# A two-layer decoder on one core: the magnitude sums of the ternary weights begin one batch earlier, two tiles per step for the first matrix

## The chip, the cores and the metric

One NeuronCore of a Trainium2 chip runs the whole program in one launch. The metric is the device time of that launch in microseconds (us). A kernel is executed several times and the median is given. One further execution is recorded by the hardware profiler; its times are the ones that the lines below show. The engines are TensorE (PE; its weight loads are listed as PEld), VectorE (DVE), ScalarE (ACT), GpSimd (POOL) and SyncE (SP), which here only issues DMAs. ACT and POOL have DMA queues of their own as well.

## The reference

Six stages over 4 batches of 512 rows by 512 features, each followed by a residual sum and a layer norm:

```python
x = _layernorm(x + _L0_attn_ref(x, ...))            # A: one head over all 512 features, rope, softmax
x = _layernorm(x + _L0_xattn_ref(x, ctx_2048, ...)) # B: 8 heads over feature blocks
x = _layernorm(x + _L0_ffn_ref(x, ...))             # C: ternary weights, 512 -> 2048 -> 512
x = _layernorm(x + _L1_attn_ref(x, ...))            # D: 16 heads
x = _layernorm(x + _L1_xattn_ref(x, ctx_2048, ...)) # E
x = _layernorm(x + _L1_ffn_ref(x, ...))             # F: 4-bit weights, 512 -> 1408 -> 512
```

The change concerns the weights of stage C. Each of its three matrices is replaced by a ternary one whose scale comes from the mean magnitude of the whole matrix:

```python
def weight_quant(w):
    scale = 1.0 / jnp.clip(jnp.mean(jnp.abs(w)), EPS)
    wq = jnp.clip(jnp.round(w * scale), -1.0, 1.0) / scale
    return w + jax.lax.stop_gradient(wq - w)

gate = bitlinear(x, w_gate)
up = bitlinear(x, w_up)
return h_bitlinear(jax.nn.silu(gate) * up, w_down)   # h_: a Walsh-Hadamard transform first
```

So a matrix has to be read once for its mean before any of it can be quantized, and it is read a second time to be quantized. The input x, the context and the weights of the other stages have no part in this.

## The kernel before

Stages are called A to F, and a task is a stage for one batch: A0, A1, ..., F3, in that order (`ORDER`). Each task is a Python generator that emits instructions for one step and yields, a step being mostly one group of matmuls into one bank of PSUM. `lanes` keeps up to two tasks going; the next one joins when the last has said "next", so that the scores and values of one batch stand beside the projections of the following. After every round `lanes` calls `step(n)`, with n the number of tasks started, and that advances the background generators of the list `BESIDE` (L40) by one step each: an entry names the task from which it runs, the last task, and a key. Key "C0" is `l0_ffn_ternary`, key ("B", 0) loads the context for B0, key "C" is `l0_ffn_weights`, which first runs what is left of "C0".

The emitted instructions then pass through a list scheduler that orders them on each engine; every engine works its queue off in that order. A `Pipe` delays a piece of work by steps: `later(n, fn)` runs fn at the nth `tick`. A statement under `issue_after(x)` isn't placed before instruction x. Tiles come from pools with a fixed number of buffers: 69 for 128x512 tiles in general ("o"), 4 for `tw` (`W_BUFS`, L28), which hold `wk`, a weight of A, first. A `tw` load thus waits until the sum of the tile four before has read its buffer.

`l0_ffn_ternary` (L579 to L634) does the following for `wg_t`, `wu_t`, `wd_t`, each 16 tiles of 128x512 float32 (256 KB):

- It loads had16 and had, two 128x128 matrices for the Walsh-Hadamard transform (had on POOL's DMA queue, L586), and casts had on DVE (L588, recorded at L60).
- Per step it loads one tile `tw` on SP (recorded at L253), and one step later `absum` sums its magnitudes on DVE (L592).
- For the second and third matrix the matrix before is quantized beside it: `fetch` reads the tile again as `tq` on ACT's DMA queue (L602), 4 steps later ACT scales it (L555), then POOL clips it (L564), ACT casts it to bf16 (`tb`, L572), and every second step a pair of tiles is stored from ACT's queue (L597).
- After 16 tiles come the row sum on DVE (L623), a matmul with ones on PE (`tot`, L627) and two small DVE instructions (L630, L631), a step apart.

`wd_t` is quantized in `l0_ffn_weights`, from B0 on, on DVE (L558, L559) and ACT (L572).

A's own names: `qk` are projections of queries and keys, `v` values, `as` scores, `ae` their exponentials, `ap` the transposed ones, `pv` the result. A float32 product is made of three matmuls of high and low parts: the split of a tile into `...h` (a cast on ACT, L144) and `...l` (L147, on DVE or POOL) is done by one helper. B reads x from DRAM as tiles `x`, makes `qh` (ACT, L471) and `ql` (DVE, L472) of it, and its scores are `bs` (PE, L528), their exponentials `be`, the transposed ones `bT`.

In A0 the task takes 4 steps of `qk`, 4 of a product of weights, 4 of `qk` and 4 of `v`, with those of its pipe, before it says "next".

Of the kernel before, what the change touches and what calls it, by code (L numbers as in the profile page):

```python
# [21 lines left out]
B, S, D = 4, 512, 512  # L22
# [14 lines left out]
F_SCALED, F_ACT, F_PAIR, F_DOWN = 1, 5, 3, 9  # L37
ORDER = "A0 A1 A2 A3 B0 B1 B2 B3 C0 C1 C2 C3 D0 D1 D2 D3 E0 E1 E2 E3 F0 F1 F2 F3"

BESIDE = [("A1", "A3", "C0"), ("A3", "B0", ("B", 0)), ("B0", "B2", "C"), ("C3", "D0", "D"), ("D1", "D3", "F0"), ("E2", "E2", "F")]  # L40


class Pipe:
# [25 lines left out]
class Net:  # L69
# [509 lines left out]
    def l0_ffn_ternary(self):  # L579


        nc = self.nc
        self.had = self.c("had", [P, P], F32R)
        self.had16 = self.load(self.c("had16", [P, P]), self.a["had16"])
        f = self.t("had")
        nc.gpsimd.dma_start(f[:, 0:P], self.a["had"])  # L586
        pipe = Pipe()
        pipe.later(3, nc.vector.tensor_copy, self.had, f[:, 0:P])  # L588

        def absum(f, part, n):  # L590
            with self.tc.issue_after(self.mark.ins):
                nc.vector.tensor_reduce(part[:, n : n + 1], f, AX.X, ALU.add, apply_absolute_value=True)  # L592


        def store(name, n, o):
            with self.tc.issue_after(self.turned.ins):
                nc.scalar.dma_start(self.tern_kept[name][n], o.bitcast(F32))  # L597

        def fetch(ap):
            f = self.o("tq")  # L600
            with self.tc.issue_after(self.turned.ins):
                nc.scalar.dma_start(f, ap)  # L602
            return f

        def keep(name, n, o):
            pipe.later(1, store, name, n, o)

        old = None
        for new in self.TERNARY:
            chunks = self.ternary_chunks(new)  # L610
            part = self.c(new + "_abs", [P, len(chunks)])
            if old:
                quant = self.ternary(pipe, old, lambda n, o, name=old: keep(name, n, o), early=True)
                todo = self.ternary_chunks(old)
            for n in range(len(chunks)):
                pipe.tick()
                pipe.later(1, absum, self.load(self.w("tw"), chunks[n][2]), part, n)
                if old:
                    pipe.later(4, quant, n, fetch(todo[n][2]))
                yield  # L620
            pipe.tick()
            m = self.c(new + "_mean", [P, 4])
            nc.vector.tensor_reduce(m[:, 2:3], part, AX.X, ALU.add)  # L623
            yield
            pipe.tick()
            ps = self.pb("tot")
            nc.tensor.matmul(ps[:, 0:1], self.ones, m[:, 2:3], start=True, stop=True)  # L627
            yield
            pipe.tick()
            nc.vector.tensor_scalar(m[:, 0:1], ps[:, 0:1], 1.0 / (len(chunks) * P * 512), 1e-5, ALU.mult, ALU.max)  # L630
            nc.vector.reciprocal(m[:, 1:2], m[:, 0:1])  # L631
            self.mean[new], self.scale[new] = m[:, 0:1], m[:, 1:2]
            old = new
        yield from pipe.drain()  # L634
# [699 lines left out]
def body(tc, args, phases=range(6)):  # L1334
    with ExitStack() as ctx:
# [9 lines left out]
        def step(n):  # L1345
            if len(phases) == 6:
                for first, last, key in BESIDE:
                    if plain.index(first) < n <= plain.index(last) + 1:
# [74 lines left out]
```

## Time and profile before

| | us |
|---|---|
| three runs | 1580.09, 1582.03, 1579.72 |
| their median | 1580.09 |
| the profiled execution | 1580.57 |
| its span on the core | 1578.9 |

The span is the time from the first to the last instruction; the profiled execution's own time is 1.7 us longer. The mean granted clock of PE is 0.994 of full speed. What the ternary weights cost one by one, in this execution:

| instruction | engine | number | mean us | where in the span |
|---|---|---|---|---|
| `tw` load (256 KB) | SP queue | 48 for the sums | lands in 3.5 to 4.0 | wg 23.0 to 99.2, wu 100.5 to 163.3 |
| L592 sum of magnitudes | DVE | 48 | 0.67 | wg 48.5 to 104.6, wu 105.8 to 169.8, wd 189.3 to 227.9 |
| L602 fetch `tq` (256 KB) | ACT queue | 32 | 0.33 to issue, lands in 4.1 (wg) and 4.8 (wu) | |
| L555 scale | ACT | 32 | 0.72 | the most of them in 160 to 242.7, the last four after 242.4 |
| L572 cast to bf16 | ACT | 32 (and 4 for wd in this stretch) | 0.62 | with those |
| L597 store | ACT queue | 16 | 0.33 to issue | |

Windows of stage A, one row per stretch: from and to, its length, the busy time of PE, PEld, DVE, ACT and POOL with the number of instructions, the granted PE clock, the share of the DMA engines, GB/s:

```profile
40.00:56.80 16.80, 16.80 (x75) 13.91 (x75) 8.66 (x12) 5.49 (x10) 14.46 (x11) 1.00 0.12 36
56.80:68.00 11.20, 11.20 (x51) 9.27 (x50) 4.12 (x7) 5.22 (x12) 8.86 (x7) 1.00 0.01 3
88.00:113.00 25.00, 25.00 (x115) 20.72 (x114) 20.26 (x34) 8.78 (x16) 15.60 (x11) 1.00 0.71 231
160.00:242.70 82.70, 80.72 (x368) 65.16 (x366) 61.54 (x100) 53.29 (x101) 66.27 (x58) 1.00 0.79 254
```

Other times in A: A0's first `as` follows the projections, and its third `as` tile starts at 67.71 us. A1's first `pv` starts at 96.81, its first `as` at 113.13, and A2's first `qk` at 124.76. The first xT tile is issued at 1.69 us and first read at 4.66. DVE waited for `tw` four times between 99.8 and 108.9 (0.64, 1.55, 0.60 and 1.01 us); L555 on ACT waited once for a `wg_t` fetch (3.8 us) and four times for `wu_t` fetches in 215 to 260 (7.1 us in all, 2.4 the longest). A3's last `ap` ends at 242.73, B0's first `bT` starts at 267.97.

### The profile page before, as it was taken

The numbers are of one execution on the slowest core, as the hardware profiler recorded it, in microseconds if no ns is written. First come the engines' busy times: TensorE is split into PE (matmuls) and PEld (weight loads), VectorE is DVE, ScalarE is ACT, GpSimd is POOL, SyncE is SP. The second block draws the span as 40 slices with busy tenths as digits, with TensorE's granted clock in tenths as the row PEclk, the third lists the DMA queues.
The fourth block names the chain that finished last, engine by engine and source line by source line (L and its number), as shares of the span: only waits on it lengthen the run. The fifth ranks groups of instructions, "written<-read, shape, count | busy, mean of one in ns | idle before, by whom it ended". The sixth has DMA issues, their size and how long they took to land.

```text
span 1578.9 us, 25669 instructions
## 1 busy us (share of the span) xinstructions
PE 1512.4 (96%) x8222; PEld 1090.9 (69%) x8222; DVE 1214.0 (77%) x2594; ACT 1041.7 (66%) x2240; POOL 687.8 (44%) x704
## 2 busy tenths in 40 slices
PE   8999998999999999999999999999999999999996
PEld 6888775555544764477777668777687677787885
DVE  6486688898876678777577797767886898888896
ACT  5334667888778877887696864969634445545554
POOL 6665783656535303430435323353324344344342
PEclk9999999999999999999999999999999999999998
DMA  7044874444224534753434345633336630020101
GB/s 256 29 160 140 266 235 151 156 165 139 71 74 126 189 132 131 208 180 130 134 101 120 103 140 148 173 96 91 130 119 220 233 113 12 20 81 1 54 1 54
DMA packets 138759, 200.72 MB, mean 127 GB/s; under 512 B 17776, under 2 KB 52592, under 8 KB 138624
## 3 DMA queue, kind: packets, MB, share of 16 engines
q1 hardware_dynamic: 127584, 178.03, 35.5%
q10 hardware_dynamic: 6912, 12.59, 2.8%
q0 software_dynamic: 4128, 8.46, 2.2%
q8 instruction: 65, 1.06, 0.3%
q14 instruction: 70, 0.57, 0.1%
HBM read 121.94 MB, written 51.90 MB: 110 GB/s over the span
## 4 chain that ended last, share of the span: by engine, by line
PE 50%; DVE 11%; ACT 9%; issue 6%; DMA 3%; POOL 2%; SPq 0%; ACTq 0%; DVEq 0%; POOLq 0%
PE fg L1238 7%; PE facc L1221 5%; DVE fg L1194 3%; PE dT L986 3%; PE dn L794 2%; PE bo L500 2%; PE pg L740 2%; ACT de L976 2%; PE pu L742 2%; PE do L1006 2%; PE bT L249 2%; PE had L808 2%; PE bs L528 2%; PE ds L961 2%; PE dq L155 1%
## 5 line engine op out<-in xcount | busy, mean ns | idle before, releaser
L1194 DVE SCALAR_TENSOR_TENSOR fg<-fg,gs,fg 128x512 f32<-128x512 f32 x220 | 163.1, 745 | 30.4 <-ACT fg L1186 15.6
L976 ACT ACTIVATE de<-de,dm 128x128 f32<-128x128 f32 (+3 forms) x256 | 142.8, 562 | 11.5 <-DVE dm L972 11.3
L1238 PE MATMUL fg<-fxh,gu 128*128 128x512 f32 x352 | 140.4, 399 | 6.2 <-DVE fg L1194 3.1
L972 DVE CUSTOM_DVE_ANT_0 de<-ds,negm,thr 128x128 f32<-128x128 f32 (+3 forms) x256 | 126.3, 546 | 18.4 <-PE ds L961 15.8
L1238 PE MATMUL fg<-fxl,gu 128*128 128x512 f32 x352 | 137.5, 391 | 0.1
L717 POOL TENSOR_TENSOR hl<-g,hh 128x512 fp32r<-128x512 f32 x64 | 83.2, 1307 | 110.8 <-ACT hh L716 90.7
L484 POOL TENSOR_SCALAR be<-be,bsm 128x512 f32<-128x512 f32 x128 | 93.4, 742 | 85.3 <-DVE bsm L482 53.7
L1198 POOL TENSOR_TENSOR fg<-fg,fg 128x512 f32<-128x512 f32 x44 | 60.1, 1367 | 140.3 <-DVE fg L1194 56.7
L478 ACT ACTIVATE be<-bs,bsm 128x512 f32<-128x512 f32 x128 | 87.3, 689 | 32.4 <-DVE bsm L476 31.0
L898 POOL TENSOR_TENSOR dql<-dqf,dqh 128x512 fp32r<-128x512 f32 x32 | 41.4, 1295 | 150.6 <-ACT dqh L897 150.5
L986 PE MATMUL dT<-ident,de 128*128 128x128 f32 x640 | 91.3, 278 | 8.4 <-ACT de L976 6.4
L986 PEld LDWEIGHTS dT<-ident,de 128*128 128x128 f32 x640 | 71.7, 141 | 27.5 <-ACT de L976 14.8
L1238 PEld LDWEIGHTS fg<-fxh,gu 128*128 128x128 f32 x352 | 66.0, 188 | 30.6 <-DVE fg L1194 13.5
L476 DVE TENSOR_REDUCE bsm<-bs 128x1 f32<-128x512 f32 x128 | 83.0, 674 | 2.3 <-PE bs L528 2.3
L249 PEld LDWEIGHTS bT<-ident,be 128*128 128x128 f32 x512 | 54.9, 141 | 29.5 <-issue 15.6
L1238 PEld LDWEIGHTS fg<-fxl,gu 128*128 128x128 f32 x352 | 66.2, 188 | 12.8 <-DVE fxl L147 0.4
L1186 ACT ACTIVATE fg<-fg,gs 128x512 f32<-128x512 f32 x88 | 60.1, 683 | 20.6 <-PE fg L1238 20.6
L249 PE MATMUL bT<-ident,be 128*128 128x128 f32 x512 | 71.2, 280 | 1.4 <-POOL be L484 0.9
L500 PE MATMUL bo<-bpT,cT 128*64 128x512 f32 x256 | 71.4, 618 | 1.0 <-ACT bpT L491 1.0
L1212 POOL TENSOR_TENSOR fhl<-fg,fhh 128x512 fp32r<-128x512 f32 x44 | 58.5, 1330 | 29.9 <-ACT fhh L1211 29.7
L740 PE MATMUL pg<-qT,tb 128*128 128x512 bf16 x256 | 66.8, 381 | 4.4 <-ACT qT L702 2.8
L1190 ACT ACTIVATE fg<-fg,gs 128x512 f32<-128x512 f32 x44 | 30.3, 689 | 60.5 <-PE fg L1238 60.4
(357 smaller groups left out, 4685.3 us busy)
## 6 DMA issues: line engine op xcount, KB each, us to landing
x<-x SPq DMA_DIRECT2D x176, 256.0 KB, 3.2
had_scratch<-hw SPq DMA_DIRECT2D x64, 256.0 KB, 2.3
z<-had_scratch SPq DMA_DIRECT2D x64, 256.0 KB, 5.9
stk<-dqh SPq DMA_DIRECT2D x192, 64.0 KB, 2.1
tw<-in_wd_t SPq DMA_DIRECT2D x32, 256.0 KB, 4.0
p<-in_gu_p SPq DMA_DIRECT2D x22, 256.0 KB, 3.1
gu_codes<-gu SPq DMA_DIRECT2D x22, 256.0 KB, 3.1
gu<-gu_codes SPq DMA_DIRECT2D x22, 256.0 KB, 4.6
```

What stands on the lines that cost most here:

```text
L249: self.nc.tensor.transpose(pt[:, i * P : (i + 1) * P], srcs[i][:, j * P : (j + 1) * P], self.ident)
L476: nc.vector.tensor_reduce(sm[:, h : h + 1], ps, AX.X, ALU.max, negate=True)
L478: nc.scalar.activation(e, ps, AF.Exp, bias=sm[:, h : h + 1], accum_out=sm[:, 2 + h : 3 + h])
L484: nc.gpsimd.tensor_scalar(es[h][i], es[h][i], sm[:, 4 + h : 5 + h], 1.0, ALU.mult, ALU.mult)
L500: nc.tensor.matmul(po[0][h * 64 : h * 64 + 64, :], cT[j][:, c : c + 64], pTs[h], start=j == 0, stop=j == NT - 1)
L717: nc.gpsimd.tensor_tensor(lo, g, hi.bitcast(F32), ALU.subtract)
L740: nc.tensor.matmul(pg, tern["wg_t"][k, c][:, m], qT[k], start=k == 0, stop=k == NT - 1)
L972: nc.vector.tensor_tensor_reduce(es[i], ps, self.negm[:, 384 - P * i :], -1.0, self.thr[:, i : i + 1], ALU.add, ALU.min, n4[:, i : i + 1])
L976: nc.scalar.activation(es[i], es[i], AF.Exp, bias=n4[:, i : i + 1], scale=-1.0, accum_out=den[:, hh * 4 + i : hh * 4 + i + 1])
L986: nc.tensor.transpose(pt[:, o + (i - j) * P : o + (i - j + 1) * P], es[i][:, j * P : (j + 1) * P], self.ident)
L1194: self.emitted["DVE"] = nc.vector.scalar_tensor_tensor(y[u], ps, s, y[u], ALU.mult, ALU.add)
L1238: nc.tensor.matmul(ps, self.gu[i, u][:, g * P : (g + 1) * P], xT[g][n], start=n == 0, stop=n == 1)
```

## The change

The background generator of the ternary weights is advanced from A0 on instead of A1. It first yields 10 times, after its loads of had16 and had. For the first matrix, `wg_t`, the pipe ticks only at even tiles and the generator yields only after odd ones, so that two tiles are loaded and summed per step. The second and third matrix go as before, one tile per step.

```diff
-BESIDE = [("A1", "A3", "C0"), ("A3", "B0", ("B", 0)), ("B0", "B2", "C"), ("C3", "D0", "D"), ("D1", "D3", "F0"), ("E2", "E2", "F")]
+BESIDE = [("A0", "A3", "C0"), ("A3", "B0", ("B", 0)), ("B0", "B2", "C"), ("C3", "D0", "D"), ("D1", "D3", "F0"), ("E2", "E2", "F")]
...
+        for _ in range(10):
+            yield
         old = None
         for new in self.TERNARY:
             chunks = self.ternary_chunks(new)
...
             for n in range(len(chunks)):
-                pipe.tick()
+                if old or n % 2 == 0:
+                    pipe.tick()
                 pipe.later(1, absum, self.load(self.w("tw"), chunks[n][2]), part, n)
                 if old:
                     pipe.later(4, quant, n, fetch(todo[n][2]))
-                yield
+                if old or n % 2:
+                    yield
             pipe.tick()
```

The 16 tiles of `wg_t` thus take steps 11 to 18 of A0, and A1 starts at about step 20. No instruction is added or removed on any engine. What the order of the engines' queues shows: had's DMA on POOL moves from 45.9 us in the profile of before to tenth place in POOL's queue, ahead of A0's work there; had's cast moves from 49.6 us to third place on DVE; `tot` for `wg_t` stands before A0's third `as` tile on PE, that for `wu_t` among A1's `ap`, that for `wd_t` in A3's `qk`. On ACT, between A3's last `v` casts and B0's `qh`, no instruction of the ternary weights is left; on DVE none between `vl` and the first `bsm` of B0.

## The prediction

> **What bounds the kernel now.** I read the page's first two parts, then the waits of TensorE (PE) over the first 300 us, then the stretches around the longest of them, then the timelines of PE and ACT there.
>
> ```profile
> PE 1512.4 (96%) x8222; PEld 1090.9 (69%) x8222; DVE 1214.0 (77%) x2594; ACT 1041.7 (66%) x2240; POOL 687.8 (44%) x704
> ...
> PE   8999998999999999999999999999999999999996
> PEld 6888775555544764477777668777687677787885
> DVE  6486688898876678777577797767886898888896
> ACT  5334667888778877887696864969634445545554
> ```
>
> PE is busy for 1512.4 of 1578.9 us, so time comes back only where PE idles or runs slowly. One slice is 39.5 us. DVE and ACT have room in slice 2 (4 and 3 tenths, 39.5 to 79 us); in the seventh, 237 to 276.3, PE has the only 8 besides the first slice and the end.
>
> ```profile
> PE qk L155 <- ACT wqh L144: 6.0, 1, 6.0
> PE bs L528 <- ACT qh L471: 3.7, 1, 3.7
> PE pv L157 <- DVE apl L147: 1.4, 2, 0.9
> PE as L156 <- DVE qkl L147: 0.5, 1, 0.5
> PE qk L156 <- POOL xTl L147: 0.5, 2, 0.3
> ```
>
> Columns: total us, times, longest. After the start, the one large wait is that of B0's first scores (`bs`) for `qh`, at the step from A3 to B0. Windows there (length; busy us of PE, PEld, DVE, ACT, POOL; granted PE clock; DMA share; GB/s):
>
> ```profile
> 238.00:242.73 4.73, 4.73 (x31) 3.97 (x29) 2.72 (x9) 2.57 (x6) 1.14 (x2) 1.00 1.01 347
> 242.73:246.44 3.71, 0.00 (x0) 0.00 (x1) 3.29 (x9) 3.71 (x8) 2.63 (x3) 0.91 0.82 165
> 246.44:249.00 2.56, 2.56 (x10) 1.77 (x12) 1.25 (x2) 1.57 (x3) 0.35 (x2) 0.50 1.04 393
> 249.00:252.30 3.30, 3.30 (x10) 2.15 (x7) 2.77 (x6) 3.30 (x8) 0.39 (x1) 0.50 0.88 294
> ...
> 320.00:440.00 120.00, 118.42 (x713) 61.85 (x714) 105.01 (x228) 100.57 (x251) 69.59 (x92) 1.00 0.34 117
> ```
>
> PE idles 3.71 us, then has half the clock for 5.86 us. The last row, B's steady state, is PE-bound at full clock, so what is saved here is saved to the end. What kept `qh`, from ACT's timeline:
>
> ```profile
> 242.40 0.72 ACT L555 ACTIVATE tq<-tq,wu_t_mean 128x512 f32<-128x512 f32 x1
> ...
> 243.03 0.62 ACT L572 ACTIVATE tb<-tq 128x512 bf16<-128x512 f32 x1
> 243.55 0.71 ACT L555 ACTIVATE tq<-tq,wu_t_mean 128x512 f32<-128x512 f32 x1
> 244.16 0.61 ACT L572 ACTIVATE tb<-tq 128x512 bf16<-128x512 f32 x1
> 244.68 0.57 ACT L144 CAST aph<-ap 128x512 fp32r<-128x512 f32 x1
> ...
> 245.15 0.72 ACT L555 ACTIVATE tq<-tq,wu_t_mean 128x512 f32<-128x512 f32 x1
> 245.77 0.62 ACT L471 ACTIVATE qh<-x 128x512 fp32r<-128x512 f32 x1
> ```
>
> Between `ap`'s end (242.73) and `qh` ACT quantizes `wu_t`; x for B0 was loaded at 171.33 and is not what is late.
>
> **Part by part.** No instruction comes or goes: each engine has the same rows in both programs. What moves is about one batch earlier: 48 `tw` loads (SP), 48 magnitude sums (L592, 0.67 us), 32 `tq` fetches and 16 stores on ACT's queue (0.33 us to issue), 32 each of L555 (0.72), L564 (POOL) and L572 (0.62), three rounds of L623, L627, L630, L631, and the load and cast of `had`.
>
> *At A3 to B0 (gain).* In the changed program ACT's order there is vh, vh, aph, qh, aph, qh, aph, qh, aph, without ternary work. Between 242.40 and `qh`'s start stand three L555 and two L572: 3×0.72 + 2×0.62 = 3.4 us. Without them the last vh ends near 242.5 (241.92 + 0.59); `aph` needs the first `ap` tile (PE, before 242), so `qh` runs from 243.1 at the latest, from 242.05 at best (right after the vh that ends there in either order). PE then idles about 0.3 us instead of 3.71 (bounds 0 and 1.0; the upper is 243.1 + 0.62 − 242.73): −3.4. The half clock follows only the long idle: 5.86 us at 0.50 lose 2.93 us; with 0.3 idle it should not come, as 0.9 us waits elsewhere (`pv` for `apl`, above) leave the clock whole: −2.9. The last bound of the gain: `ap`'s end to the first `bT` takes 25.24 us, in which 6 score groups of 0.89 and 4 `pv` tiles of 2.95 need 17.1, so 8.1 us at most can come back here; 6.3 are named, and of the other 1.8 (waits for `apl` and single `bs`, whose ACT part also thins) I take 0.5. Sum −6.8; bounds −8.1 and 0 (if something else is as late).
>
> *What is late next.* After `qh`, `ql` (DVE 0.68) and `aph`/`apl`. DVE has no L558/559 in between any more, only vl and apl, so `ql` of the first group is there within 1 us of `qh`; a remaining stall of that size is in the bounds.
>
> *A0 (cover).* 16 sums are 16×0.67 = 10.8 us of DVE in 40 to 62 us, where DVE is idle 8.1 of 16.8 (40.00:56.80) and 7.1 of 11.2 (56.80:68.00). Four `tw` buffers and 3.5 us to land pace them: the mean is ready near 62.6, its PE `tot` stands in PE's order before the third `as` tile, 67.7 before: about 5 us to spare. DVE's next, `asm`, is some 1.75 us late in that stretch and is absorbed by the idle time. If the cover is gone, PE waits at `tot`: price its lateness, 0 here, up to 2 if tiles land twice as slowly (3.5 → 7).
>
> *A1 (the risk).* Here `wg_t` is fetched and quantized and `wu_t` summed. SP's `tw` loads pass x-transposed loads, and ACT's queue gets fetches ahead of the casts of A2's xT. DVE does ten sums in a row (6.7 us) paced by the four buffers, ending near 104; then `apl` at 105 to 106.3, which PE wants at 107. On ACT the two L555 of the first fetches wait for DMA (`tq` takes 4.1 us: issued 104.7 and 106.6, usable 108.8 and 110.7), and three casts queue behind them; they end at 112.6 to 113.7 and PE wants them at 114.5 and 115.2. Slack 0.2 to 1.6 us: I take +0.5, bounds 0 and 4 (two waits, each 2 us longer, as the longest wait of an L555 for its fetch in 215 to 260 was 2.4). This kind of clog exists in before between A2 and A3: 160 to 242.7 holds 80.72 of 82.7 PE-busy, 2.0 us. It moves into A1/A2 and leaves A3: net 0, bounds −2 and +2.
>
> The row for transfers is 238.00:242.73, share 1.01 at 347 GB/s, with `tq` landing in 4.1 to 4.8 us and `tw` in 3.5. The Trainium skill, "Trainium Kernel Development and Optimization", section "Key Constraints", says that transfers from SP's, ACT's and POOL's queues share 16 engines and interleave; that speaks against this change, since A1 already shows 0.71 share (88.00:113.00) and gets `tq` on top. By that rule alone the 0.5 would be an estimate of 1 to 2 us.
>
> *Start.* `had` (64 KB, POOL queue, 0.73 us to issue, 2.2 to land) and had16 go out ahead of the first loads; 128 KB at 350 GB/s (as 347 above) are 0.37 us, half of it in the first loads' way: +0.2. Its cast (L60, 0.22 us) is now DVE's third instruction, ahead of wql (5.99 in before); the DMA goes out at 1.5 to 2.2 and lands at 4.4, or 7.1 at the slowest (4.9, had16's): blocks DVE 0 to 1.3 us. I take 0.
>
> *B0, B1.* wd's quantization begins sooner and two L558/L559 pairs (0.9 us each) leave B's steady stretch, where DVE is busy 105.01 of 120 and PE bounds: 0, bounds −0.5 and 0.
>
> Sum: −6.8 + 0.5 + 0 + 0.2 + 0 = −6.1. Against the profiled execution (1580.57; span 1578.9 and 1.7 around it) 1574.5; the median, 1580.09, is 0.5 lower, so about 1574.3 between the two readings.
>
> **On the clock.** The row is 3.71 us idle, then 5.86 us at 0.50. The Trainium skill, "TensorE: Matmul & The Clock Gate", "Part 1: The HAM clock gate", has the clock halved after an idle window of about 3.4 us and whole again after about as long busy. By it the half clock would cost an estimated 1.7 us instead of 2.9 and the total would be near 1575.5.
>
> **Rivals.** A measurement here can tell about 0.2% from no change: 3.2 us, so 1576.9 and 1583.3 are the limits.
>
> 1. *The gain is given back.* Either `qh` or `ql` is late for another reason (A3's last `ap` casts, four `apl` on DVE in a row), or one stall in A1 is long enough to halve the clock too: 3.7 + 2.9 = 6.6. For: A1's slack is at most 1.6 us. Against: ACT has no ternary work at the step, and a 6.6 needs the casts 3.7 us later than I make them. −6.1 + 2 to −6.1 + 6.6: 1576.5 to 1581, centre 1579.
> 2. *ACT's queue clogs twice (the slower side).* Fetched tiles come late in A1 and again in A2, each time ACT stands at L555 while xT's casts wait behind it, PE idles 3.7 us or more and gets half the clock: 2×6.6 − 6.1 = +7.1, 1587.5. It decides from where A2's and A3's first xT casts come 3.7 us after PE wants them. For: an L555 in before waited 3.8 us for a `wg_t` fetch, and 7.1 in four waits for `wu_t`. Against: the same load on A2 and A3 in before cost 2.0 us up to 242.7, without half clock.
> 3. *Nothing changes at B0*, because the list order is kept: excluded by the changed order of ACT; only as part of rival 1.
>
> **How the numbers follow.** Forecast 0.68 (own range 1571.5 to 1576.9), rival 1 0.16, rival 2 0.16. Of rival 1, 0.03 lies below 1576.9, 0.11 within the limits and 0.02 above; of rival 2 0.14 above and 0.02 within. Faster 0.71, same 0.13, slower 0.16. Range 1571.5 (the −8.1 of the transition, plus 0.2, minus 0.7 elsewhere) to 1582: 0.05 lies below, 0.15 above.
>
> **What would show it.** Right: the PE wait for `qh` under 1 us, no window at 0.50 around 240, first `bT` about 18 to 20 us after the last `ap`, `tot` for `wg_t` without a wait in A0, and PE waits of 0 to 2 us in 88 to 125. Wrong: a wait of PE over 3 us or a clock under 0.9 in A1 or A2, a first `qk` more than 1 us later than before, or ACT waiting for `tq` with xT's casts behind it.

## The result and the profile after

The changed kernel is slower, by about half a per cent. Its five times are 1584.96, 1587.43, 1589.93, 1593.87 and 1594.07 us, median 1589.93, against 1580.09 of five runs of the kernel before beside them: ratio 1.0061, 95% interval 1.0033 to 1.0088. Measured again, it gave 1584.42 against 1577.02, ratio 1.0046 (1.0031 to 1.0062); both intervals lie above 1. Why the first five times spread over 9 us stays open. The forecast was 1574.3, faster.

The profiled execution (1584.96) has a span of 1583.2 us. From its page, busy time and the slices, as for the kernel before:

```profile
PE 1512.2 (96%) x8222; PEld 1091.7 (69%) x8222; DVE 1222.8 (77%) x2594; ACT 1039.6 (66%) x2240; POOL 688.2 (43%) x704
...
PE   8999899999999999899999999999999999999996
...
DVE  6685787888876688877567797767786888888896
```

PE has the same 1512 us of work. The 8 of the seventh slice (237 to 277 us) is a 9 now, and the fifth (158 to 198) has become an 8. The 8 of the seventeenth is no effect of the change: a second profile of the kernel before (r_before below) has it as well. PE's waits in the first 300 us (total us, times, longest):

```profile
PE qk L155 <- ACT wqh L144: 6.9, 2, 6.4
PE as L156 <- DVE qkl L147: 5.1, 3, 3.8
PE pv L157 <- DVE apl L147: 4.0, 2, 3.4
PE as L155 <- ACT qkh L144: 0.7, 1, 0.7
PE pv L155 <- ACT aph L144: 0.3, 1, 0.3
PE bs L528 <- DVE ql L472: 0.2, 1, 0.2
```

The wait of 3.7 us for `qh` has become one of 0.2 for `ql`. In its place stand two of 3.8 and 3.4 us, for low parts that DVE makes: `qkl` (low part of the projected queries and keys, for A2's scores) and `apl` (low part of A2's transposed exponentials, for `pv`, beside A3's projections). Windows of the changed kernel around them (length; busy PE, PEld, DVE, ACT, POOL; granted clock; DMA share; GB/s):

```profile
170.00:175.00 5.00, 4.93 (x22) 3.75 (x20) 5.00 (x6) 2.14 (x5) 4.84 (x4) 1.00 0.83 264
175.00:180.00 5.00, 0.58 (x2) 0.27 (x2) 5.00 (x8) 3.42 (x8) 4.67 (x6) 0.79 0.83 280
180.00:185.00 5.00, 5.00 (x12) 3.85 (x13) 3.61 (x7) 1.53 (x3) 4.76 (x6) 0.52 0.82 228
...
220.00:225.00 5.00, 3.93 (x17) 2.60 (x15) 5.00 (x5) 3.25 (x6) 5.00 (x4) 1.00 0.78 237
225.00:230.00 5.00, 2.38 (x6) 1.90 (x7) 4.27 (x6) 1.25 (x3) 5.00 (x5) 0.57 0.36 135
230.00:235.00 5.00, 5.00 (x18) 4.01 (x17) 4.88 (x7) 0.98 (x2) 5.00 (x4) 0.74 0.00 0
```

In both places DVE is busy for all or nearly all of the time and POOL too, PE idles, and afterwards PE works some 5 us at half the clock (the traces have it at 0.50 from 177.9 to 184.8 and from 225.7 to 232.6). What was one late tile at the step from A3 to B0 has become two. The step itself is clean, as ACT's timeline of the changed kernel shows:

```profile
254.96 0.59 ACT L144 CAST vh<-v 128x512 fp32r<-128x512 f32 x1 [2.08 <-PE v L157]
255.44 0.60 ACT L144 CAST aph<-ap 128x512 fp32r<-128x512 f32 x1
255.92 0.64 ACT L471 ACTIVATE qh<-x 128x512 fp32r<-128x512 f32 x1
```

To see where time went, PE's timeline is cut at the first `ap` transpose of each batch and at B0's first `bT`. The table has both kernels, each in two profiles (the second ones are r_before and r_after below), in us:

| stretch | before | again | after | again | after − before |
|---|---|---|---|---|---|
| start to A0's first `ap` | 81.3 | 80.7 | 82.0 | 81.3 | +0.6 to +0.7 |
| to A1's | 42.8 | 42.8 | 45.5 | 46.2 | +2.7 to +3.4 |
| to A2's | 72.4 | 72.5 | 77.9 | 79.5 | +5.5 to +7.0 |
| to A3's | 44.0 | 43.7 | 49.3 | 49.2 | +5.3 to +5.5 |
| to B0's first `bT` | 27.3 | 27.2 | 19.2 | 19.2 | −8.0 to −8.1 |
| the rest | 1310.9 | 1309.4 | 1309.2 | 1308.8 | −1.7 to −0.6 |

The gain at the step was had in full, 8 us. It was paid for with 14 to 17 us in A0 to A3, and A2 and A3 are the larger part.

### The profile page after: what moved, and what is told of

It reads as the page before. It is cut to its first block, busy times and chain, and to the rows that moved or that the text cites. A ratio compares the mean times of both kernels' runs of the same rounds, so it can differ in the third digit from the quotient of the medians.

```text
span 1583.2 us, 25665 instructions
## 1 busy us (share of the span) xinstructions
PE 1512.2 (96%) x8222; PEld 1091.7 (69%) x8222; DVE 1222.8 (77%) x2594; ACT 1039.6 (66%) x2240; POOL 688.2 (43%) x704
## 4 chain that ended last, share of the span: by engine, by line
PE 57%; DVE 16%; ACT 12%; issue 7%; DMA 4%; POOL 3%; SPq 0%; ACTq 0%; DVEq 0%; POOLq 0%
PE fg L1243 7%; PE facc L1226 5%; PE dT L991 3%; DVE fg L1199 3%; PE bo L500 2%; ACT de L981 2%; PE pg L745 2%; PE dn L799 2%; PE bT L249 2%; PE pu L747 2%; PE do L1011 2%; PE ds L966 2%; ACT be L478 2%; PE bs L528 1%; DVE bsm L476 1%
## 5 line engine op out<-in xcount | busy, mean ns | idle before, releaser
L991 PEld LDWEIGHTS dT<-ident,de 128*128 128x128 f32 x640 | 71.7, 141 | 27.5 <-ACT de L981 14.8
```

Of the source, the lines that this page charges most:

```text
L991: nc.tensor.transpose(pt[:, o + (i - j) * P : o + (i - j + 1) * P], es[i][:, j * P : (j + 1) * P], self.ident)
```

## The experiments

Theory D: DVE works its queue in order, and what the change puts in front of the splits that PE waits for (sums, scalings) costs, by its length or because its tile has not landed. Rival P: POOL's rope products (those of `z` with the rotary factors, and their sums) set the pace in A2 and A3, and DVE would wait for them anyway. Each kernel was compared with the kernel before on its chip; these have medians from 1576.7 to 1578.5 us. All in one table, in us; the stretches are those above, each from its batch's predecessor (A1 is "to A1's first `ap`"), and come from one profile each:

| kernel | median | ratio to before (95%) | A1 | A2 | A3 | step | rest |
|---|---|---|---|---|---|---|---|
| e1_hold_wd | 1578.57 | 0.9999 (0.9984 to 1.0014) | 50.3 | 77.3 | 42.9 | 19.4 | 1308.2 |
| e2_short_wd_sums | 1588.49 | 1.0070 (1.0043 to 1.0098) | 47.0 | 79.8 | 47.4 | 19.3 | 1308.4 |
| e3_short_wu_clips | 1584.03 | 1.0041 (1.0029 to 1.0052) | 46.2 | 79.6 | 47.3 | 19.2 | 1311.0 |
| e4_first_only | 1584.84 | 1.0043 (1.0028 to 1.0059) | 42.7 | 72.3 | 49.5 | 27.6 | 1309.6 |
| e5_hold_lag3 | 1580.84 | 1.0021 (1.0009 to 1.0033) | 46.8 | 79.4 | 42.9 | 19.3 | 1310.4 |
| e6_hold_sp_fetch | 1579.04 | 1.0009 (0.9997 to 1.0021) | 46.3 | 74.1 | 45.8 | 19.3 | 1311.2 |
| e8_before_late_quant | 1578.01 | 1.0004 (0.9994 to 1.0015) | 42.8 | 73.3 | 45.1 | 19.3 | 1315.0 |
| e9_hold_k18 | 1577.77 | 1.0003 (0.9992 to 1.0014) | 43.0 | 80.3 | 43.0 | 19.3 | 1313.1 |
| r_after | 1584.42 | 1.0046 (1.0031 to 1.0062) | 46.2 | 79.5 | 49.2 | 19.2 | 1308.8 |
| f1_hold_lag3_k18 | 1578.15 | 1.0003 (0.9993 to 1.0012) | 43.0 | 74.5 | 48.0 | 19.4 | 1309.0 |
| f2_hold_lag3_sp | 1580.93 | 1.0025 (1.0014 to 1.0035) | 46.7 | 76.9 | 46.9 | 19.3 | 1308.0 |
| f3_lag3_short_both | 1592.9 (one execution) | | 48.0 | 74.2 | 60.4 | 19.3 | 1308.0 |
| g1_two_early | 1581.32 | 1.0030 (1.0018 to 1.0042) | 45.1 | 72.5 | 44.1 | 28.9 | 1306.8 |
| g2_hold_k22 | 1584.96 | 1.0055 (1.0038 to 1.0073) | 44.0 | 77.7 | 48.0 | 20.1 | 1312.1 |
| g3_hold_wg_fetch_late | 1581.27 | 1.0027 (1.0014 to 1.0040) | 42.7 | 80.1 | 46.8 | 19.3 | 1308.0 |
| r_before | 1578.19 | 1.0002 (0.9989 to 1.0016) | 42.8 | 72.5 | 43.7 | 27.2 | 1309.4 |
| h1_before_pairs4_hold | 1578.81 | 1.0010 (0.9996 to 1.0023) | 42.8 | 72.5 | 45.5 | 21.5 | 1312.0 |
| h2_before_pairs8_hold | 1575.93 | 0.9994 (0.9983 to 1.0005) | 42.9 | 72.4 | 43.9 | 25.4 | 1309.0 |

### A3: wd_t's scaling

```diff
+                with self.tc.issue_after(self.low[False].ins):
-                nc.vector.tensor_scalar(f, f, self.scale[name], MAGIC, ALU.mult, ALU.add)
+                    nc.vector.tensor_scalar(f, f, self.scale[name], MAGIC, ALU.mult, ALU.add)
```

> The changed kernel, with the first scaling of each wd_t tile (L558 of the changed kernel) not placed before the last high/low split on DVE that was emitted before it; this takes four pairs of L558/L559 out of A3's projections (207 to 214 us in the changed kernel, 6.8 us of DVE there) and leaves the rest of DVE's order as it is. Theory D (DVE is too full in A2 and A3): PE's wait of 3.4 us for apl near 224 goes to under 1 us, the half clock at 225 to 232 goes, and the span falls by 4 to 6 us against the changed kernel's profiled 1583.2. Rival P (POOL's rope products set the pace there, DVE would wait for them anyway): a wait of 2.5 us or more stays and the span moves by less than 2.

The wait for `apl` near 224 is gone, A3 falls from 49.3 to 42.9 us, and the median is that of the kernel before, 6 to 11 us under the changed kernel's. The order of all engines up to the end of A3 is otherwise that of the changed kernel, so the whole loss of A3 is these four pairs. ("The held kernel" is this one below.) The span fell by 3.2 where 4 to 6 were expected, because this profile's A1 was 4.8 us longer than the changed kernel's first. That isn't the edit's doing, since A1 has the same order: here two fetches landed 0.9 and 1.9 us later, PE waited 1.6 us for `qkh` where it had not waited, and its clock was at half from 119.8 to 126.6. DVE's timeline of the changed kernel shows what the hold took away:

```profile
207.53 2.94 DVE L558 TENSOR_SCALAR tw<-tw,wd_t_mean 128x512 f32<-128x512 f32 x2
210.39 2.27 DVE L559 TENSOR_SCALAR tw<-tw 128x512 f32<-128x512 f32 x2
212.59 0.86 DVE L558 TENSOR_SCALAR tw<-tw,wd_t_mean 128x512 f32<-128x512 f32 x2
213.37 0.75 DVE L559 TENSOR_SCALAR tw<-tw 128x512 f32<-128x512 f32 x2
```

Two scalings take 2.94 us while POOL works on the rope products and 0.86 when it does not. They are emitted in B0, but `wd_t`'s mean is ready at 203 us in the changed kernel, where it came at 241.6 before, and the scheduler places them in A3.

### A2: sums, clips, late tiles

Two cuts, each on the changed kernel: the sums of `wd_t` over 8 of 512 columns, and POOL's clips of `wu_t` on 8 of 512; the rest of that work is left out.

```diff
+                g = f[:, 0:8] if "wu_t" in self.scale else f
-                nc.vector.tensor_reduce(part[:, n : n + 1], f, AX.X, ALU.add, apply_absolute_value=True)
+                nc.vector.tensor_reduce(part[:, n : n + 1], g, AX.X, ALU.add, apply_absolute_value=True)
```

> The changed kernel, with the 16 magnitude sums of wd_t taken over 8 of the 512 columns (most of their work is left out; loads, order and waits stay). Theory D: seven of these sums stand before the split qkl that PE waits 3.8 us for at 176 to 180; without them the wait is under 1.2 us, the half clock at 180 to 185 goes, and the span falls by 4 to 6 us. Rival P: qkl is late because POOL's join of the rope products is late; the wait stays above 2.5 us and the span falls by less than 2.

```diff
+                g = f[:, 0:8] if name == "wu_t" else f
-                nc.gpsimd.tensor_scalar(f, f, MAGIC + 1.0, MAGIC - 1.0, ALU.min, ALU.max)
+                nc.gpsimd.tensor_scalar(g, g, MAGIC + 1.0, MAGIC - 1.0, ALU.min, ALU.max)
```

> The changed kernel, with POOL's 16 clips of wu_t (L564) done on 8 of the 512 columns (the rest of wu_t stays unclipped). Rival P: POOL is busy for 31 of 40 us in 160 to 200, so without the clips the joins come earlier, PE's wait for qkl in 170 to 185 falls under 1.2 us and the span by 4 to 6. Theory D: the wait stays above 2.5 us, the span falls by less than 2.

Neither helped: the wait for `qkl` was 5.6 us with the short sums, and 3.3 plus 2.8 with the short clips. Both theories fail as they were put. DVE's timeline of e2_short_wd_sums tells why the first one did:

```profile
177.18 0.21 DVE L593 TENSOR_REDUCE wd_t_abs<-tw 128x1 f32<-128x8 f32 x2
182.04 0.16 DVE L593 TENSOR_REDUCE wd_t_abs<-tw 128x1 f32<-128x8 f32 x1 [4.65 <-DMA tw<-in_wd_t]
182.12 0.98 DVE L147 TENSOR_TENSOR qkl<-z,qkh 128x512 fp32r<-128x512 f32 x1
```

The sum itself is 0.16 us now, but it stands ahead of `qkl` in DVE's queue and waits 4.65 us for its tile. With full sums DVE is busy over the same stretch:

```profile
172.49 3.79 DVE L236 TENSOR_SCALAR x<-x,ln 128x512 f32<-128x512 f32 x3
176.20 0.67 DVE L147 TENSOR_TENSOR vl<-v,vh 128x512 fp32r<-128x512 f32 x1
176.80 1.86 DVE L592 TENSOR_REDUCE wd_t_abs<-tw 128x1 f32<-128x512 f32 x3
178.57 1.28 DVE L147 TENSOR_TENSOR qkl<-z,qkh 128x512 fp32r<-128x512 f32 x1
```

(changed kernel.) So the theory was widened (W): an entry whose tile has not landed counts as much as one that takes long. Tests on the held kernel: sums of the second and third matrix emitted three steps after their loads; second reads issued by SP.

```diff
-                pipe.later(1, absum, self.load(self.w("tw"), chunks[n][2]), part, n)
+                pipe.later(3 if old else 1, absum, self.load(self.w("tw"), chunks[n][2]), part, n)
...
+            for _ in range(2 if old else 0):
+                pipe.tick()
+                yield
             pipe.tick()
             m = self.c(new + "_mean", [P, 4])
```

> The held kernel (e1_hold_wd) with the magnitude sums of wu_t and wd_t emitted three steps after their loads instead of one, so that on DVE none stands ahead of the splits while its tile is still on its way. Theory W (DVE and ACT work in order, and a sum or a scaling whose tile has not landed holds up the splits behind it): PE's wait for qkl in A2's scores, 4.8 us with e1_hold_wd, goes under 1.5 us, and the median falls by 3 to 5 us against e1_hold_wd, to 1573 to 1576. Rival P (POOL's joins of the rope products are late of themselves): a wait over 2.5 us stays and the time moves by less than 2 us.

```diff
-                nc.scalar.dma_start(f, ap)
+                nc.sync.dma_start(f, ap)
             return f
```

> The held kernel (e1_hold_wd) with the 32 second reads of wg_t and wu_t issued from SP's queue instead of ACT's. Theory W: in A1 the first two fetches are issued only at 106 to 109 us because ACT waited 9.6 us for PE ahead of them; from SP they go out earlier, the first two scalings (L555) wait under 1 us together instead of 7.4, and what A1 loses up to A2's first projection (3 to 7 us) falls under 2. Rival Q (SP's queue is held up as well, by loads that wait for a free buffer): the scalings wait 3 us or more, loads of x or x-transposed come later and the time is 2 us or more above e1_hold_wd.

With the later sums the waits for `qkl` fell to 1.5 and 0.7, but 2.5 us for `xTl` from POOL came after them and halved the clock: A2 stayed at 79.4 and the time did not fall, a miss. With SP's fetches A2 fell to 74.1 (wait 1.9). A1 took 46.3, as in the changed kernel: its wait for `apl` grew to 1.7, and a scaling on ACT still waited 6.4 us for its tile, since SP issued that fetch only at 108.8; this too is a miss. The time is within noise of e1_hold_wd. Together:

> The held kernel with both changes of before, the second reads from SP's queue and the sums three steps after their loads. Theory W: the waits add up to under 4 us between 100 and 240 (8.2 with e1_hold_wd, 7.7 with e6_hold_sp_fetch, 7.7 with e5_hold_lag3), the first bT comes at 263 to 266 us, and the time is 1574 to 1577. Rival: DVE's and POOL's work in A1 and A2 is what is too much, whatever the queue; the waits stay at 6 us or more and the time at 1578 to 1581.

A2 76.9, a wait of 3.6 for `qkl` again, waits of 7.7 in all, 1580.93: the rival's numbers. And all at once, late sums, short sums, short clips, without the hold:

> The changed kernel (without the hold on wd_t's scaling) with the sums of wu_t and wd_t three steps after their loads, the sums of wd_t over 8 of the 512 columns and POOL's clips of wu_t on 8 of 512 columns; most of the work of these sums and clips is left out. Cutting one of the two alone left PE's wait for qkl in A2 at 5.6 and 6.0 us. Theory W+P (sums, clips and late tiles hold up the same chain, so that each alone only uncovers the next): the waits between 170 and 190 add up to under 1 us, while that for apl near 224 stays over 2 us, since wd_t's scaling still stands in A3. Rival: something else is late there (x-transposed tiles, ACT), and over 2.5 us stay.

2.1 us were left in A2, where under 1 was expected. A3 took 60.4 us; PE's line there, and DVE's before it:

```profile
236.79 0.79 PE L157 MATMUL pv<-vh,apl 128*128 128x512 f32 x1 [12.52 <-DVE apl L147]
```

```profile
226.38 2.88 DVE L558 TENSOR_SCALAR tw<-tw,wd_t_mean 128x512 f32<-128x512 f32 x2
229.19 2.89 DVE L559 TENSOR_SCALAR tw<-tw 128x512 f32<-128x512 f32 x2
232.00 1.48 DVE L558 TENSOR_SCALAR tw<-tw,wd_t_mean 128x512 f32<-128x512 f32 x1
...
234.65 1.48 DVE L559 TENSOR_SCALAR tw<-tw 128x512 f32<-128x512 f32 x1
236.05 0.68 DVE L147 TENSOR_TENSOR apl<-ap,aph 128x512 fp32r<-128x512 f32 x1
```

Here the four pairs, at 1.5 us for each instruction, stand right in front of the last `apl`: e1_hold_wd's finding again, larger.

That A2's loss is the third matrix's work at all is shown by leaving the second where the change has it and only sending the third back, 18 empty steps after the second:

```diff
             old = new
+            if new == "wu_t":
+                for _ in range(18):
+                    pipe.tick()
+                    yield
```

> The changed kernel with 18 empty steps after the second matrix: wg_t and wu_t are summed as in the changed kernel and wg_t quantized as there, wu_t is quantized and wd_t summed as late as in the kernel before. Theory D (the loss in A2 is the third matrix's sums and the second's quantization standing there, that in A3 wd_t's scaling): A1 loses 2 to 3 us up to A2's first projection as in the changed kernel (127.5 to 128.5 there), then A2 loses nothing, PE's waits between 165 and 235 stay under 2 us together, and the wait for qh at the step to B0 is back with 3 to 4 us; time 1579 to 1583. Rival: A2's wait follows from A1 being late, and over 3 us of it stay.

A1 45.1, A2 72.5 as before, the step back at 28.9 with a wait of 5.5 us for `qh` (3 to 4 were expected). The rest is as expected, and the rival falls. DVE's busy time over 30 us around A2's scores is 21.5 before (150 to 180 us) and 28.8 after (154 to 184), POOL's 25.5 and 27.5; sums of the windows, before and then after:

```profile
sum 30.00, PE 28.95 PEld 22.70 DVE 21.48 ACT 15.67 POOL 25.45; mean PE 4.83 PEld 3.78 DVE 3.58 ACT 2.61 POOL 4.24
```

```profile
sum 30.00, PE 25.51 PEld 20.34 DVE 28.75 ACT 15.59 POOL 27.53; mean PE 4.25 PEld 3.39 DVE 4.79 ACT 2.60 POOL 4.59
```

Which piece of that work holds `qkl` stays open: sums, clips, late tiles and POOL's splits took one another's place. Counted from `ap` to `ap`, A2 has 14 magnitude sums in both kernels, but 22 scalings, 21 clips and 22 casts after where 16, 16 and 14 stood before. The number alone does not set the loss: e6_hold_sp_fetch has 14 sums, 19 scalings, 20 clips and 20 casts there and takes 74.1.

### A1: fetches ahead of the casts

```diff
             old = new
+            if new == "wg_t":
+                for _ in range(18):
+                    yield
```

> The changed kernel, with 18 empty steps after the first matrix, so that wg_t is summed in A0 as in the changed kernel while wu_t and wd_t are summed and wg_t and wu_t quantized in the steps of the kernel before. Theory D: the loss comes from the second and third matrix moving, so here only the start's 0.4 us is lost, PE waits for qh at the step from A3 to B0 by 3 to 4 us as before, and the time is 1579 to 1582. Rival S (the sums in A0 and their transfers are what costs): 1584 or more, with PE late by 2 us or more at A1's first scores.

A1 and A2 are as before, 42.7 and 72.3, so the sums in A0 cost nothing but the start: rival S falls. The time is 1584.84 all the same, the rival's number and a miss, but from another place: A3 takes 49.5. There the sums of `wd_t` and the fetches and scalings of `wu_t` stand in another order than before, a sum waits 2.7 us for its tile with `qkl` behind it, a cast on ACT 4.3 us for `kf` (a tile of B's context), and PE waits 1.8 for `aph` and 2.3 for `apl`. ACT's timeline of the changed kernel in A1:

```profile
105.05 0.62 ACT L144 CAST qkh<-z 128x512 fp32r<-128x512 f32 x1 [9.57 <-PE v L156]
105.94 0.33 ACTq L602 DMA_DIRECT2D tq<-in_wg_t  x1
...
107.26 0.37 ACTq L602 DMA_DIRECT2D tq<-in_wg_t  x1
111.59 0.73 ACT L555 ACTIVATE tq<-tq,wg_t_mean 128x512 f32<-128x512 f32 x1 [4.21 <-DMA tq<-in_wg_t]
113.70 0.72 ACT L555 ACTIVATE tq<-tq,wg_t_mean 128x512 f32<-128x512 f32 x1 [1.38 <-DMA tq<-in_wg_t]
114.33 1.12 ACT L144 CAST xTh<-xT 128x512 fp32r<-128x512 f32 x2
```

ACT stands 9.6 us at a cast that a matmul of PE's `v` releases (in the kernel before a cast stood 10.1 us there too, with no fetch behind it); only then do the fetches go out, and ACT stands at their scalings with `xTh` and `qkh` behind. Moving the fetches 10 steps later, the sums left alone:

```diff
+                    go = lambda n=n, quant=quant, todo=todo: pipe.later(4, quant, n, fetch(todo[n][2]))
-                    pipe.later(4, quant, n, fetch(todo[n][2]))
+                    if old == "wg_t":
+                        pipe.later(10, go)
+                    else:
+                        go()
```

> The held kernel (e1_hold_wd) with the second reads of wg_t and their quantization 10 steps later, the sums where they are. Theory T (in A1 ACT stands at scalings whose tile is still on its way, the casts of x-transposed and the splits behind it): A2's first projection comes under 126.5 us (132.5 with e1_hold_wd, 127.9 in the changed kernel, 124.8 before) and the only wait left in A1 is that for apl, under 1.2 us. Rival D1 (the ten sums of wu_t in a row on DVE are what costs A1): 127.5 or later.

A2's first `qk` came at 125.8 us and A1 at 42.7: the ten sums in a row, which are still there, were not the matter; the fetches and scalings of `wg_t` were, by the waits on ACT that the timeline shows. The work then stood in A2 (80.1), where PE waited 2.7 us for `xTh`.

### Smaller shifts, and the gain alone

With 18 and 22 empty steps at the start (for 10), on the held kernel, and 18 with the later sums:

```diff
-        for _ in range(10):
+        for _ in range(18):
             yield
```

> The held kernel (e1_hold_wd) with 18 empty steps at the start in place of 10, so that the sums of wg_t end in A1 and the second and third matrix move 10 steps instead of 18. Theory W: only where the sums and fetches fall against the batch's scores counts; ACT's order at the step from A3 to B0 is as clean as with 10, and A1 gets no fetch before its scores, so the waits in A1 fall under 1.5 us; the time is 1572 to 1577. Rival (any earlier start costs the same 5 to 8 us in A2 and A3): 1579 to 1584.

> The held kernel with 18 empty steps (e9_hold_k18) and the sums of the second and third matrix three steps after their loads. With e9_hold_k18 DVE waited 4.8 us for a tile of wd_t at 167.7, the splits behind it, and PE 5.2 us for qkl. Theory W: DVE waits for no tile, PE's wait there is under 1.5 us, the first bT comes at 262 to 264 us (267.7 with e9_hold_k18, 268.0 before). If stage B passes that on, the time is 1572 to 1574; if it takes most of it back, as it did with e8_before_late_quant, 1575 to 1578. Rival P (POOL): the wait stays above 3 us.

> The held kernel with 22 empty steps, so that the second and third matrix move 6 steps. Theory D: A1 and A2 are as in the kernel before or lose under 2 us, ACT has two casts of wu_t left before the values of A3, none between them and qh, and the first bT comes at 261 to 265 us (268.0 before); the time 1573 to 1577. Rival: a wait of 3 us or more in A2 as with 18 steps, time 1577 to 1580.

None came within its expected time, the first two by under 1 us. In the first (1577.77) a sum waited 4.8 us for its tile and PE 5.2 for `qkl` (A2 80.3); the later sums removed this (74.5), and A3 lost 3.1 to `apl` behind a sum that waited 2.2 us. With 22, A1's `ap` waited 3.5 for exponentials and A3's values 2.5. Each shift has its pile-up elsewhere; none beats the kernel before.

The gain alone, in the kernel before: the last 8 tiles of `wu_t` fetched and quantized 14 steps later; then the third matrix by pairs of tiles, from the fifth and from the ninth (the second diff; 8 for 4 in the last):

```diff
+                    go = lambda n=n, quant=quant, todo=todo: pipe.later(4, quant, n, fetch(todo[n][2]))
-                    pipe.later(4, quant, n, fetch(todo[n][2]))
+                    if old == "wu_t" and n >= 8:
+                        pipe.later(14, go)
+                    else:
+                        go()
```

```diff
+                pair = new == "wd_t" and n >= 4
-                pipe.tick()
+                if not pair or n % 2 == 0:
+                    pipe.tick()
...
-                yield
+                if not pair or n % 2:
+                    yield
```

> The kernel before, with only the last 8 tiles of wu_t fetched and quantized 14 steps later, in B0, so that ACT has no ternary work between A3's last value casts and B0's first qh; nothing is moved earlier. This prices the gain of the step from A3 to B0 by itself. Theory G (that step is worth 6 to 8 us and the changed kernel paid for it in A1 to A3): PE's wait for qh under 1 us, no half clock after it, first bT 17 to 19 us after the last ap, the time 1571 to 1575. Rival B (the wait comes back in B0, where the quantization now stands, or the gain was never there): 1577 to 1582.

> The kernel before, with two tiles per step from the fifth tile of wd_t on (its sums and wu_t's quantization end 6 steps sooner) and wd_t's first scaling held behind the splits as in e1_hold_wd; A0 to A2 are untouched. Theory D (only what stands in front of PE's splits costs): A1 and A2 as in the kernel before (42.9 and 72.4 us from the first ap of one batch to that of the next), A3 44 to 46, the step to B0 19 to 20 instead of 27.4; the first bT at 260 to 263 us and the time 1570 to 1574. Rival: pairs of tiles in A3 overfill DVE, ACT and POOL there, A3 takes 48 us or more and the time is 1575 to 1580.

> As the run above, but with pairs only from the ninth tile of wd_t on (4 steps sooner); DVE's order up to the end of the sums is then that of the kernel before, and two casts of wu_t still stand between the first and second qh. Theory D: A3 44 to 45 us, the step to B0 20 to 22, the first bT at 261 to 264 us, the time 1571 to 1575. Rival: A3 48 us or more, or the step still 25, the time 1576 to 1580.

The first took the step to 19.3 us and `bT` to 261.9, 6.1 earlier than in the first profile of the kernel before and 4.9 than in the second; from there to stage C's first `pg` product it took 195.4 us where the kernel before took 190.0 and 191.4, and the median did not move: the gain is real, and B, where the eight quantizations now stand, took most of it back. The second had the step at 21.5 and `bT` 4.7 earlier, the third 25.4 and 3.1. All three missed their times: none has an interval below 1, and the best, 0.9994, is no difference. Why the 3 to 5 us of the last two do not show is not settled; up to the first `pg` they still had 2.3 and 2.7 us, and twelve times of one kernel scatter over 6 to 8.

> The kernel before once more, for a second profile. Theory G: the wait for qh at the step to B0 is there again with 3.5 to 4 us and the half clock after it, and the first bT at 267 to 269 us; what differs between two profiles of one kernel comes from stage C on. Rival: the wait in the first profile was one of a scatter, and here it is under 2.5 us, which would explain why taking it away did not show in the median of e8_before_late_quant.

> The changed kernel once more, unaltered, for a second profile and more times. Its first five times lay between 1584.96 and 1594.07, those of the kernel before within 3.3 us. Theory H (waits of PE of 3 to 4 us, each of which halves its clock or just does not): the same two waits, for qkl near 176 and for apl near 224, of 3 to 5 us each, plus the wait in A1, their sum larger than the 8.7 us of the first profile if the time is larger. Rival: the waits in A1 to A3 are as in the first profile and the scatter comes from later stages.

The second profiles repeat the first: 3.8 us for `qh` before; 4.8 for `qkl` and 3.4 for `apl` after. Of the 2.7 us between the two profiles of the kernel before, 1.2 lie ahead of B0's first `bT`, where none was expected.

## Why the prediction was wrong

- *What bounds the kernel, and that only waits and the clock of PE count:* right. The same 1512 us of PE work before and after.
- *The step from A3 to B0, −6.8 with bounds −8.1 and 0:* right in mechanism, and too small: −8.0 to −8.1 (−7.9 from A3's last `ap`, as the prediction counts: 25.24 us before, 17.33 after). Of the 1.8 us of which it took 0.5, 1.6 came. `qh` follows `aph` at once, the half clock is gone, and nothing else was late there.
- *Start +0.2, A0 at nothing:* +0.6 to +0.7 together; no wait for `tot`. The start is 0.4 of it (first `qk` at 6.4 us for 6.0).
- *A1 +0.5, bounds 0 and 4:* right in mechanism, +2.7 to +3.4. The mis-sized term is the landing of the two fetches that ACT waits for: 4.1 us were taken, 5.6 and 6.4 it was, and they were issued 1.2 and 0.7 us later than assumed, so the scalings could start at 111.6 and 113.7 where 108.8 and 110.7 stood in the sum. With the same order in A1, e1_hold_wd's profile lost 7.5 us there, beyond the bound of 4, with half the clock, which rival 1 had named.
- *"It moves into A1/A2 and leaves A3: net 0, bounds −2 and +2":* the first step that failed. A2 lost 5.5 to 7.0. The clog of the kernel before was taken as a thing that moves with its batch and keeps its price. In the kernel before twelve sums of `wu_t` and the quantization of `wg_t` stand in A2, which takes 72.4 us; with `wd_t`'s sums and `wu_t`'s quantization there instead, and what is left of `wg_t`'s, it takes 77.9 and 79.5, and with those two sent back 72.5 (g1_two_early). So this work costs A2 5 to 7 us, at waits for `qkl` of 3.8 and 4.8 with half the clock after. Which part of it, and in what order against the splits, is not shown. The prediction's own sign of being wrong, a wait over 3 us or a clock under 0.9 in A2, is what came.
- *"B0, B1: wd's quantization begins sooner and two L558/L559 pairs leave B's steady stretch: 0":* the second that failed. The pairs were costed in B, where the source emits them; in the order of DVE's queue the first four stand in A3's projections, before A2's last `apl`, and take 6.6 us of DVE there. Price: A3's 5.3 to 5.5 us, all of it (e1_hold_wd).
- *What is saved at the step goes to the end:* mostly. The rest after the first `bT` is 1307 to 1313 us in all runs that put no more work into B, and 1315.0 in the one that did.
- *Rival 2, two stalls with half clock, 1587.5:* its size and its clock are what came (1582 to 1594), its place is not: DVE in A2 and A3, not ACT waiting for fetches in A1 and A2. That its number fits is luck. Its chance of 0.16 was weighed by the load on transfers; DVE's queue and POOL were not counted against it, though DVE was busy for 61.5 and POOL for 66.3 of the 82.7 us from 160 on.

## What to carry to other kernels

Work that is moved earlier under a scheduler must be priced in the order of each engine's queue, not where the source emits it: everything that depends on it (here the scaling behind the mean) moves too, as far as the scheduler lets it. In an in-order queue an entry costs its own time and the time its input is late, and the entries behind it pay; look for the splits and casts that stand behind it. Where several engines are nearly full (here PE, DVE and POOL at 85, 96 and 92% of the 30 us around A2's scores), cutting one cause only uncovered the next; taking a whole piece of work out of the stretch, as g1_two_early did, told more.

## What the runs showed of the hardware

A DVE instruction's time depends on what POOL does beside it. L558, 0.48 us in B0, took up to 1.52 us each in A3 beside POOL's rope products; the split `qkl`, 0.68 alone, up to 1.77; the layer norm's L236 1.26 (3.79 for three) where 0.54 is its time alone. The sum L592 (one input, a reduction) took 0.65 to 0.69 in every stretch, and the splits `vl` and `apl`, which have one input in PSUM, 0.65 to 0.69 as well, in all runs (the short sums of two runs aside). The Trainium skill, "GPSIMD Engine Reference", section "1. Specifications", says that GpSimd shares its SBUF interfaces with VectorE and contends with DVE instructions in a two-port mode or with two SBUF inputs; the rows agree for the split `qkl` with both inputs in SBUF and for the untouched sum, `vl` and `apl`, and which mode L558 and L236 run in no row here shows.

Between 20 and 300 us the granted clock of PE is either full or half in these traces, and a stretch at half lasts 3.41 us or a multiple of it: 6.83 us after the wait of the kernel before (245.7 to 252.6) and after both of the changed kernel, 13.65 us with the wait of 12.5 in f3_lag3_short_both. All 13 waits of PE of 3.38 us or more in that stretch had it. Shorter ones had it in part: those of 1.2 us in e2_short_wd_sums (109.0 to 110.2, half from 110.5) and 2.0 in f2_hold_lag3_sp (108.3 to 110.2, half from 110.7) did, those of 2.1 in h1_before_pairs4_hold and 2.8 in e6_hold_sp_fetch did not. So the length of a single wait does not tell it below 3.4 us. An estimate from these figures: the price of such a wait is open by 1.7 to 3.4 us, half of 3.41 or 6.83, as far as PE has work in that time.
